# Two graph-attention layers: layer 1's probabilities turned by DMA blocks and VectorE instead of TensorE

## The chip, the cores and the metric

The kernel runs on one core of a Trainium2 chip, in one launch. The time is the device time of that core in microseconds (us), the median of several executions. One further execution was taken by the hardware profiler; its page and trace are what this text reads. Engines are named as in the profile: PE is TensorE, DVE is VectorE, ACT is ScalarE, POOL is GpSimd, and SP is the engine that issues DMAs.

## The reference, cut to what matters

The input is 128 graphs of 64 nodes with 768 features, and a 0/1 adjacency per graph. Layer 0 is a 12-head graph attention with a gate; the change doesn't touch it. Layer 1 is a 6-head self-attention, masked by the adjacency, with head size 128:

```python
def _L1_gnn_ref(seq_inputs, Wq, bq, Wk, bk, Wv, bv, Wf, bf, graph_mask):
    q = _heads(seq_inputs @ Wq + bq)
    k = _heads(seq_inputs @ Wk + bk)
    v = _heads(seq_inputs @ Wv + bv)
    scores = jnp.einsum('bhqd,bhkd->bhqk', q, k) / np.sqrt(HEAD_SIZE)
    bias = jnp.where(graph_mask, 0.0, NEG)[:, None]
    probs = jax.nn.softmax(scores + bias, axis=-1)
    ctx = jnp.einsum('bhqk,bhkd->bhqd', probs, v)
    ctx = ctx.transpose(0, 2, 1, 3).reshape(...)
    return ctx @ Wf + bf
...
x = _layernorm(x + _L1_gnn_ref(x, ..., adj), axis=-1)
```

Everything is float32. The softmax comes out with the query node on the partitions. For the contexts TensorE sums over the key node, so the probabilities are needed with the key node on the partitions: they must be transposed, 64 by 64 for each graph and head.

## The kernel before, in words

**Tiles.** A tile is two graphs, 128 rows. There are 64 tiles, 32 pairs of tiles, and in layer 1 16 groups of two pairs (four tiles). Within a group, q (0 or 1) is the pair and i (0 or 1) the tile of the pair. Layer 0 (`phase_a`) runs first and leaves in DRAM, for each tile, its output `x1_d`, the same transposed (`xT_d`), and layer 1's values `v_d`. Then `phase_b` does layer 1.

**Dense products.** The four large products use a bilinear algorithm with 15 half-size products: `STEPS` lists 15 steps, each with two float32 products of 128 by 128 by 256, which the profile shows as four MATMULs of line 428. A `Stream` object holds one such pass. In each step VectorE (line 1205 for q and k, 1222 for the last product) or ScalarE (line 1200) adds the partial sum from PSUM to its outputs. PSUM has four buffers for this (`psX`) and four more for everything else in the layer (`psb`).

**Order of the work.** There is no planner at run time. `phase_b` puts closures into a dictionary under a step number, `run` calls them in that order, and each engine's instruction queue, and SP's queue of DMAs, is filled in just this order. An instruction waits on semaphores for its inputs and buffers; what stands behind it on the same engine waits with it. Step numbers are therefore positions in the queues, not times, and an engine that has little to do runs ahead.

**One window.** Group g starts at step o = 90 g. In 90 steps the queue holds 15 steps of q for even heads, 15 of k for even heads, 15 of q and 15 of k for odd heads (steps o to o+59, `start_qk`), and the output product of the group before (steps o+60 to o+89, `start_f`, 15 for each pair). After step o+62 stand the scores (line 1244), read out by VectorE with the mask added (line 1253). The softmax of group g runs in the window of group g+1: with o' = o + 90, it starts at step `sm` = o' + 5. For tile (q, i) the start is t = sm + 3 i + 8 q, and then

- t: row maximum (line 1265), t+1: subtraction (1284), both on VectorE
- t+3: exponential on ScalarE (1287), t+6: row sum on VectorE (1291)
- t+7: reciprocal on VectorE (1295) and scaling on GpSimd (`sm_scale`, line 1296), in place
- t+4: the four DMAs that load this tile's values from `v_d` (`load_v`, line 1159), into one of three places of `xb`, taken in turn, so that the fourth tile's load waits for the contexts of the first pair
- t+10: `probs`: three TensorE transposes of 128 by 128 into PSUM (line 1302) and a ScalarE copy to SBUF, into `pt` (line 1308)
- t+12, for i = 1: `contexts` of the pair: 192 small matmuls (line 1326), then four VectorE reads that add the bias of v (line 1340).

From the contexts GpSimd forms the eleven sums that the output product needs (`pair_sum`, line 1190), from step sm + 18 for the first pair. The last group has no following window; it uses its own schedule, with the exponential per head on ScalarE.

**Tiles' places.** q and k of a group are held in two tiles each (`start_qk`, name with `bufs=2`), one for even and one for odd heads; the scores read them at step o+62. The next group's k for odd heads is written from step o'+45 on.

**DMAs.** All of layer 1's DMAs stand in SP's queue. SP issues them one after the other; if one must wait, SP waits. Stores of the finished x (line 1356) wait for ScalarE's normalization; loads of x (1166), of the transposed input (485) and of the adjacency (1144) stand there too.

Of the kernel before, what the change touches and what calls it, by code (L numbers as in the profile page):

```python
# [10 lines left out]
F32 = mybir.dt.float32  # L11
U8 = mybir.dt.uint8
AF = mybir.ActivationFunctionType
ALU = mybir.AluOpType
AX = mybir.AxisListType

P = 128
# [204 lines left out]
def kernel(  # L222
# [31 lines left out]
    nc = tc.nc  # L254
# [869 lines left out]
    def phase_b(ctx, wq, wk, early_sums):  # L1124
# [11 lines left out]
        DUP = {0: 0, 2: 1, 4: 2, 5: 3}  # L1136
        bv_v = bv_c.rearrange("p (j h) -> p j h", h=2)
        st = [dict() for _ in range(NG)]

        def load_adj(g):  # L1140
            d = st[g]
# [51 lines left out]

        def start_qk(d, name, w, bias, j):

            o = k1.tile([P, 6, 2, P], F32, name=name, bufs=2)

            def first(b, positive, ps):
                hd = 2 * (b % 3) + j
                nc.scalar.activation(  # L1200
                    o[:, b], ps, AF.Identity, bias=bias[:, hd : hd + 1], scale=1.0 if positive else -1.0
                )

            def add(b, positive, ps):
                nc.vector.tensor_tensor(o[:, b], o[:, b], ps, ALU.add if positive else ALU.subtract)  # L1205

            d[name] = Stream(
                lambda r, slot, c: w[:, slot, c, j * P : (j + 1) * P],
                lambda r, slot, c: (
                    dup[:, DUP[r]] if d is st[0] and r in DUP else group_part(d, r)  # L1210
                )[:, :, c, :],
                [P, 2, P],
                first,
                add,
            )
            d[name + "T", j] = o
# [33 lines left out]
        def scores_read(d, nb):  # L1250
            for q in range(2):
                for i in range(2):
                    nc.vector.scalar_tensor_tensor(
                        d["s"][q][:, i, 2 * nb : 2 * nb + 2, :], d["pc", nb][:, q, i],
                        1.0 / math.sqrt(DH),
                        d["fill"][:, q, i, None, :].to_broadcast([P, 2, S]),
                        op0=ALU.mult, op1=ALU.add,
                    )
# [34 lines left out]
        def sm_scale(d, q, i):  # L1293
            s, rs = sm_part(d, q, i), small.tile([P, HEADS], F32, name="rs1")
            nc.vector.reciprocal(rs, d["sm", q, i])
            nc.gpsimd.tensor_tensor(s, s, rs[:, :, None].to_broadcast([P, HEADS, S]), ALU.mult)

        def probs(d, q, i):

            ps = psb.tile([P, CH, P], F32, name="pb")  # L1300
            for j in range(CH):
                nc.tensor.transpose(  # L1302
                    ps[:, j, :],
                    d["s"][q][:, i, 2 * j : 2 * j + 2, :].rearrange("p h m -> p (h m)"),
                    ident,
                )
            d["pt", i] = spare[i].rearrange("p (c n) -> p c n", n=P)
            nc.scalar.copy(d["pt", i], ps)

        def contexts(d, q):  # L1310
            pcs = [context(d, q, i) for i in range(2)]
# [100 lines left out]
        for g in range(NG):  # L1412
            d, o = st[g], N * g
            d["S"] = {} if g else early_sums
            last = g == NG - 1
            if g:
                at(o - 29 if g > 1 else 14, lambda g=g: load_T4(g))
                at(o - 35, lambda g=g: load_adj(g))
            at(o + 26, lambda d=d: fill(d))
            ready = {}  # L1420
            for k in sorted(range(len(SUMS)), key=need) if g == 0 else range(len(SUMS)):

                if g == 0:

                    if k > 3:
                        at(max(int(need(k)) - 5, 0), lambda d=d, k=k: sum_of_group(d, k, nc.vector))
                    continue
                if g == 1:

                    t = max([R * 3 + SUM_STEPS[k] + 2] + [ready[r] for r in SUMS[k][:2] if r in ready])  # L1430
                    ready[6 + k] = t
                else:
                    t = o - 24 + 2 * k
                at(t, lambda d=d, k=k: sum_of_group(d, k, nc.gpsimd))
            if g == 0:
                for r, n in DUP.items():
                    nc.scalar.copy(dup[:, n], group_part(d, r))
            for j in range(2):
                for n, (name, w, bias) in enumerate((("q", wq, bq_c), ("k", wk, bk_c))):
                    b0 = o + (2 * j + n) * R  # L1440
                    at_first(b0, lambda d=d, a=(name, w, bias, j): start_qk(d, *a))
                    for i in range(R):
                        at_first(b0 + i, lambda d=d, name=name, i=i: d[name].step(i))
            b0 = o + 4 * R + 2
            at(b0, lambda d=d: scores(d))
            for nb in range(3):
                at(b0 + 1 + (1 if last else 2) * nb, lambda d=d, nb=nb: scores_read(d, nb))

            sm = o + 4 * R + 6 if last else o + N + 5
            for q in range(2):  # L1450
                f = o + ((6 if last else 10) + q) * R
                for i in range(2):

                    t = sm + 4 * i + 13 * q if last else sm + 3 * i + 8 * q
                    at(t + (2 if last else 4), lambda g=g, q=q, i=i: load_v(g, q, i))
                    if last:
                        at(t, lambda d=d, q=q, i=i: sm_top(d, q, i, True))
                        at(t + 2, lambda d=d, q=q, i=i: sm_top_exp(d, q, i))
                        at(t + 5, lambda d=d, q=q, i=i: sm_scale_act(d, q, i))
                        at(t + 8, lambda d=d, q=q, i=i: probs(d, q, i))  # L1460
                        if i:
                            at(t + 11, lambda d=d, q=q: contexts(d, q))
                        continue
                    at(t, lambda d=d, q=q, i=i: sm_top(d, q, i))
                    at(t + 1, lambda d=d, q=q, i=i: sm_sub(d, q, i))
                    at(t + 3, lambda d=d, q=q, i=i: sm_exp(d, q, i))
                    at(t + 6, lambda d=d, q=q, i=i: sm_total(d, q, i))
                    at(t + 7, lambda d=d, q=q, i=i: sm_scale(d, q, i))
                    at(t + 10, lambda d=d, q=q, i=i: probs(d, q, i))
                    if i:  # L1470
                        at(t + 12, lambda d=d, q=q: contexts(d, q))

                pr = sm + (6 + 13 * q if last else 8 + 8 * q)
                ready = {}
                for k in range(len(SUMS)):
                    if q == 0:
                        t = pr + 10 + (k if last else 2 * k)
                    else:

                        t = max(  # L1480
                            [f - R + SUM_STEPS[k] + 1, pr + 10]
                            + [ready[r] for r in SUMS[k][:2] if r in ready]
                        )
                        ready[6 + k] = t
                    at(t, lambda d=d, q=q, k=k: pair_sum(d, q, k))
                at(f - (3 if last else 12), lambda g=g, q=q: load_x(g, q))
                at(f - (1 if last else 8), lambda d=d, q=q: add_bf(d, q))
                at_first(f, lambda d=d, q=q: start_f(d, q))
                for i in range(R):
                    at_first(f + i, lambda d=d, q=q, i=i: d["F", q].step(i))  # L1490
                if last and q:
                    for b in range(6):
                        t = f + max(i for i in range(R) if STEPS[i][5][b])
                        at(t, lambda d=d, b=b: end_stats(d, b))

                    at(f + R - 2, lambda d=d: end_top(d, 1))
                    at(f + R - 1, lambda d=d: end_top(d, 0))
                    at(f + R - 1, lambda g=g, d=d: end_norm(g, d, 1))
                    at(f + R - 1, lambda g=g, d=d: end_norm(g, d, 0))
                    continue  # L1500
                for i in range(2):
                    t = f + R + 1 + 2 * i
                    at(t, lambda d=d, q=q, i=i: norm1(d, q, i))
                    at(t + 1, lambda d=d, q=q, i=i: norm2(d, q, i))

                    at(t + 4 + 2 * i, lambda d=d, q=q, i=i: norm3(d, q, i))
                    at(t + 6 + 2 * i, lambda g=g, d=d, q=q, i=i: store(g, d, q, i))
            if g == 0:
                at(16, lambda: load_adj(0))
                bf_bc = rows(k1, bf, "bf_bc")  # L1510
# [40 lines left out]
```

## Time and profile before

| what | value |
|---|---|
| median of 3 executions | 2821.89 us (2819.24 to 2822.54) |
| profiled execution, its own time | 2821.93 us |
| span of the profiled execution | 2820.1 us, mean granted clock of TensorE 0.995 |
| busy share: PE, DVE, ACT, POOL | 98%, 68%, 41%, 53% |
| layer 1, one window: length, PE busy | 85.73 us, all of it |
| line 1302, transposes of layer 1 | 192 instructions, 273 ns each |
| line 1308, copies from PSUM | 64 instructions, 478 ns each |
| line 1296, scaling on GpSimd | 60 instructions, 828 ns each |

The span runs from the first to the last instruction; the execution's own time is 1.8 us longer, and stands within 0.1 us of the median. A matmul's duration in the profile overlaps that of the next one, so what an instruction costs TensorE is read from the distance between starts. The DMA records give for each DMA the start and length of its issue on SP, the start of each packet, and the moments at which its parts completed.

### The profile page before, as it was taken

To read this page: it belongs to the slowest core of one execution; us is meant where nothing else is said; L and a number is where in the kernel's file an instruction comes from. 1 tells how busy PE (TensorE), PEld (TensorE's weight loads), DVE (VectorE), ACT (ScalarE), POOL (GpSimd) and SP (SyncE) were. 2 spreads that over 40 slices of the span, in tenths; PEclk is the share of its full clock that TensorE was granted. 3 is DMA by queue.
4 is the path that set the end of the run, shared out by engine and by line. 5 is a ranking of instruction groups with operands and counts; after the bars stand their busy time and mean duration, and the time that the engine had idled before them with its cause. 6 is when DMAs were issued, how large, how long until landed. Compare 5 with 4: busy or idle time off the path is not lost.

```text
span 2820.1 us, 50020 instructions
## 1 busy us (share of the span) xinstructions
PE 2775.9 (98%) x17544; PEld 1958.7 (69%) x17544; DVE 1905.0 (68%) x4026; ACT 1163.1 (41%) x3685; POOL 1495.9 (53%) x1791
## 2 busy tenths in 40 slices
PE   8899999999999999999799999999999999999998
PEld 7445545555555555555578888888888888888887
DVE  4888888888888888888754555555555555555556
ACT  4466565665666665665622221122221222211223
POOL 1656556555555565565455645445645445554455
PEclk9999999999999999999899999999999999999999
DMA  5454454454454454444631221221221222211222
GB/s 147 126 151 136 136 152 130 133 154 131 133 157 134 133 150 132 140 150 132 174 130 35 91 81 65 70 91 58 91 73 63 80 65 84 91 68 58 91 85 74
DMA packets 358682, 308.36 MB, mean 109 GB/s; under 512 B 226592, under 2 KB 304160, under 8 KB 358432
## 3 DMA queue, kind: packets, MB, share of 16 engines
q1 hardware_dynamic: 358144, 304.77, 35.2%
q8 instruction: 140, 2.29, 0.3%
q14 instruction: 110, 0.90, 0.1%
q10 hardware_dynamic: 288, 0.39, 0.0%
HBM read 191.41 MB, written 101.06 MB: 104 GB/s over the span
## 4 chain that ended last, share of the span: by engine, by line
PE 93%; DVE 3%; DMA 1%; POOL 1%; ACT 1%; SPq 0%; issue 0%; POOLq 0%; DVEq 0%; ACTq 0%
PE X L428 70%; PE X L373 15%; PE pa L901 2%; PE pb L1326 2%; PE pb L1244 2%; PE pa L883 1%; PE pb L1302 1%; PE X L715 1%; PE X L700 1%; POOL Sc L1190 0%; DMA w<-in_L_gnn_Wv_dram 0%; DVE s L853 0%; ACT s L862 0%; DMA hb_bc<-in_L_gnn_H_b_dram 0%; DVE T L634 0%
## 5 line engine op out<-in xcount | busy, mean ns | idle before, releaser
L428 PE MATMUL X<-S,w 128*128 128x256 f32 x2752 | 636.5, 380 | 0.0
L428 PE MATMUL X<-w,S 128*128 128x512 f32 (+1 forms) x1364 | 598.9, 584 | 10.7 <-POOL S L668 7.5
L428 PEld LDWEIGHTS X<-S,w 128*128 128x128 f32 x2752 | 519.1, 190 | 68.5
L428 PEld LDWEIGHTS X<-w,S 128*128 128x128 f32 x1364 | 254.9, 191 | 289.8 <-issue 241.0
L1222 DVE TENSOR_TENSOR xs<-xs,X 128x256 f32<-128x256 f32 x512 | 209.6, 418 | 175.1 <-PE X L428 166.9
L872 POOL TENSOR_TENSOR s<-s,rs 128x384 f32<-128x384 f32 x128 | 106.9, 836 | 372.1 <-DVE rs L870 355.9
L428 PE MATMUL X<-w,Sc 128*128 128x256 f32 x1280 | 294.4, 381 | 0.1
L1205 DVE TENSOR_TENSOR k<-k,X 128x256 f32<-128x256 f32 x320 | 132.6, 417 | 232.4 <-PE X L428 160.6
L373 PE MATMUL X<-w,S 128*128 128x384 f32 x768 | 270.9, 490 | 1.5 <-POOL S L456 1.4
L428 PEld LDWEIGHTS X<-w,Sc 128*128 128x128 f32 x1280 | 241.5, 190 | 34.1 <-DVE xs L1222 0.9
L1205 DVE TENSOR_TENSOR q<-q,X 128x256 f32<-128x256 f32 x320 | 132.9, 419 | 195.0 <-PE X L428 155.0
L428 PE MATMUL X<-xb,w 128*128 128x256 f32 x1024 | 258.6, 383 | 0.8 <-ACT q L1200 0.8
L862 ACT ACTIVATE s<-s,nmx 128x64 f32<-128x64 f32 x768 | 254.8, 335 | 6.8 <-DVE nmx L857 6.8
L516 ACT ACTIVATE xs<-xs,shift,rstd 128x768 f32<-128x768 f32 x62 | 63.5, 1025 | 435.8 <-POOL shift L512 416.0
L428 PE MATMUL X<-w,T 128*128 128x512 f32 (+1 forms) x496 | 223.9, 583 | 5.7 <-DVE xb L757 3.4
L1200 ACT ACTIVATE k<-X,bk_c 128x256 f32<-128x256 f32 x192 | 90.9, 473 | 316.4 <-PE X L428 316.4
L846 ACT ACTIVATE s<-s,src 128x64 f32<-128x64 f32 x768 | 196.6, 338 | 37.6 <-DMA s<-dst_d 34.2
L428 PEld LDWEIGHTS X<-xb,w 128*128 128x128 f32 x1024 | 192.2, 190 | 28.4 <-ACT q L1200 1.2
L757 DVE TENSOR_TENSOR hgp<-hgp,X 128x512 f32<-128x512 f32 (+1 forms) x235 | 150.6, 651 | 80.8 <-PE X L428 67.2
L1200 ACT ACTIVATE q<-X,bq_c 128x256 f32<-128x256 f32 x192 | 90.8, 473 | 276.7 <-PE X L428 276.7
L373 PEld LDWEIGHTS X<-w,S 128*128 128x128 f32 x768 | 141.1, 190 | 90.1 <-POOL S L456 1.6
L1190 POOL TENSOR_TENSOR w<-cT 128x256 f32<-128x256 f32 x32 | 23.3, 727 | 334.2 <-PE X L428 332.9
(143 smaller groups left out, 4893.1 us busy)
## 6 DMA issues: line engine op xcount, KB each, us to landing
xb<-in_x_dram SPq DMA_DIRECT2D x64, 384.0 KB
s<-dst_d SPq DMA_DIRECT2D x128, 192.0 KB
x_d<-xb SPq DMA_DIRECT2D x64, 384.0 KB
xT_d<-T SPq DMA_DIRECT2D x64, 384.0 KB
v_d<-v SPq DMA_DIRECT2D x128, 192.0 KB
xb<-xT_d SPq DMA_DIRECT2D x32, 768.0 KB
xb<-v_d SPq DMA_DIRECT2D x256, 96.0 KB
xs<-x_d SPq DMA_DIRECT2D x64, 384.0 KB
```

The costliest lines, as they stand in the source:

```text
L373: nc.tensor.matmul(o, self.lhsT(i, c), rhs, start=first and c == 0, stop=last and c == CH - 1, skip_group_check=True,)
L428: nc.tensor.matmul(ps, self.lhsT(r, slot, c), self.rhs(r, slot, c), start=start and c == 0, stop=stop and c == 1, skip_group_check=True,)
L516: nc.scalar.activation(r, r, AF.Identity, bias=shift, scale=rstd)
L757: nc.vector.tensor_tensor(o, o, view(ps), ALU.add if positive else ALU.subtract)
L846: nc.scalar.activation(self.s[:, a], self.s[:, a], AF.Prelu, bias=self.src[:, a : a + 1], alpha=LEAKY_ALPHA,)
L862: nc.scalar.activation(self.s[:, a], self.s[:, a], AF.Exp, bias=self.nmx[:, a : a + 1], accum_out=self.sm[:, a : a + 1],)
L872: nc.gpsimd.tensor_tensor(t, t, rs[:, :, None].to_broadcast([P, A // 2, S]), ALU.mult)
L901: nc.tensor.matmul(self.pos[h2][own, j, :], self.pt[rws, j, own], rhs, start=True, stop=True,)
L1200: nc.scalar.activation(o[:, b], ps, AF.Identity, bias=bias[:, hd : hd + 1], scale=1.0 if positive else -1.0)
L1205: nc.vector.tensor_tensor(o[:, b], o[:, b], ps, ALU.add if positive else ALU.subtract)
L1222: nc.vector.tensor_tensor(o, o, ps, ALU.add if positive else ALU.subtract)
L1244: nc.tensor.matmul(pc[own, q, i, j, :], qT[:, b, q, own], kT[:, b, q, own], start=True, stop=True,)
```

## The change: what it does

The transposition is taken apart into two moves. A 64-by-64 transposition is four 32-by-32 blocks, each transposed in itself, with the two off-diagonal blocks changing places. VectorE transposes 32-by-32 blocks inside a group of 32 partitions (`nc.vector.transpose`); bringing blocks to other partitions is left to DMA, by way of a DRAM tile.

For the groups 0 to 14 (the last one keeps the old way):

- `scores_read` writes the heads in another order (slot h*3 + j instead of 2j + h), so that the blocks of one half are contiguous.
- `sm_scale` writes its product to a new place, `turned`, with the two halves of the key nodes outermost.
- `probs` is replaced by `probs_out` at t+10: one DMA of 192 KB from `turned` to the DRAM tile `p_d`, in 512 runs of 384 bytes, and four DMAs of 48 KB back into `blocked`, each to 32 partitions in 128 runs of 384 bytes; and by `probs_turn` at t+20: one VectorE transposition of 128 by 384 from `blocked` into `pt`. The three TensorE transposes and the ScalarE copy are gone.
- `contexts` moves from t+12 to t+22. With t now sm + 3 i + 11 q, the first pair's contexts move from o'+20 to o'+30, the second's from o'+28 to o'+41. The pair sums move with them.
- `load_v` no longer follows t: the first three tiles are loaded at sm, sm+1 and sm+2, the fourth at sm+26.
- `turned` and `blocked`, two of each, lie in the tile that holds k for odd heads (`late`), which is free from step o+62 until the next group's k for odd heads is written.

```diff
+        late = k1.tile([P, 6, 2, P], F32, name="k1")
+        parts = late.rearrange("p b q n -> p (b q n)").rearrange("p (t f) -> p t f", t=4)
+        turned = [parts[:, i].rearrange("p (b h m) -> p b h m", b=2, m=32) for i in range(2)]
+        p_d = [spill.tile([4, P, CH * 32], F32, name=f"p_d{i}") for i in range(2)]
+        blocked = [parts[:, 2 + i].rearrange("p (g j m) -> p g j m", g=4, m=32) for i in range(2)]
...
-            o = k1.tile([P, 6, 2, P], F32, name=name, bufs=2)
+            o = late if (name, j) == ("k", 1) else k1.tile([P, 6, 2, P], F32, name=name + str(j))
...
         def scores_read(d, nb):
             for q in range(2):
                 for i in range(2):
+                    own = d["s"][q][:, i]
                     nc.vector.scalar_tensor_tensor(
-                        d["s"][q][:, i, 2 * nb : 2 * nb + 2, :], d["pc", nb][:, q, i],
+                        own[:, 2 * nb : 2 * nb + 2, :] if d is st[-1]
+                        else own.rearrange("p (h j) m -> p h j m", h=2)[:, :, nb],
+                        d["pc", nb][:, q, i],
...
         def sm_scale(d, q, i):
             s, rs = sm_part(d, q, i), small.tile([P, HEADS], F32, name="rs1")
             nc.vector.reciprocal(rs, d["sm", q, i])
-            nc.gpsimd.tensor_tensor(s, s, rs[:, :, None].to_broadcast([P, HEADS, S]), ALU.mult)
+            d["sn", i] = turned[i]
+            nc.gpsimd.tensor_tensor(
+                turned[i].rearrange("p b h m -> p h b m"),
+                s.rearrange("p h (b m) -> p h b m", b=2),
+                rs[:, :, None, None].to_broadcast([P, HEADS, 2, 32]),
+                ALU.mult,
+            )
...
+        def probs_out(d, q, i):
+
+            nc.sync.dma_start(
+                p_d[i].rearrange("q p x -> p q x"),
+                d["sn", i].rearrange("p b (h j) m -> p (b h) (j m)", h=2),
+            )
+            for h in range(2):
+                for b in range(2):
+                    o = 32 * (2 * h + b)
+                    nc.sync.dma_start(
+                        blocked[i][o : o + 32].rearrange("p g j m -> p g (j m)"),
+                        p_d[i][2 * b + h].rearrange("(g n) x -> n g x", g=4),
+                    )
+
+        def probs_turn(d, i):
+            d["pt", i] = spare[i].rearrange("p (c n) -> p c n", n=P)
+            nc.vector.transpose(
+                d["pt", i].rearrange("p c (g n) -> p c g n", g=4),
+                blocked[i].rearrange("p g j m -> p j g m"),
+            )
...
-                    t = sm + 4 * i + 13 * q if last else sm + 3 * i + 8 * q
-                    at(t + (2 if last else 4), lambda g=g, q=q, i=i: load_v(g, q, i))
+                    t = sm + 4 * i + 13 * q if last else sm + 3 * i + 11 * q
+                    at(t + 2 if last else sm + (2 * q + i if 2 * q + i < 3 else 26), lambda g=g, q=q, i=i: load_v(g, q, i))
...
-                    at(t + 10, lambda d=d, q=q, i=i: probs(d, q, i))
+                    at(t + 10, lambda d=d, q=q, i=i: probs_out(d, q, i))
+                    at(t + 20, lambda d=d, i=i: probs_turn(d, i))
                     if i:
-                        at(t + 12, lambda d=d, q=q: contexts(d, q))
-
-                pr = sm + (6 + 13 * q if last else 8 + 8 * q)
+                        at(t + 22, lambda d=d, q=q: contexts(d, q))
+
+                pr = sm + (6 + 13 * q if last else 18 + 11 * q)
```

## The prediction

> **What bounds the kernel now.** First the page: TensorE is busy for 98% of the span and carries 93% of the chain that ended last.
>
> ```profile
> span 2820.1 us, 50020 instructions
> PE 2775.9 (98%) x17544; PEld 1958.7 (69%) x17544; DVE 1905.0 (68%) x4026; ACT 1163.1 (41%) x3685; POOL 1495.9 (53%) x1791
> ```
>
> A mean over both layers says little, so next a table of stretches of layer 1 (length, busy time by engine, clock, DMA share, GB/s), and the chain, from which I take the scores of two successive groups.
>
> ```profile
> 1772.00:1858.00 86.00, 86.00 (x693) 75.46 (x687) 46.82 (x126) 18.64 (x36) 43.34 (x53) 1.00 0.22 75
> ...
> 2154.95 2.95 PE pb L1244 x96
> ...
> 2240.68 2.95 PE pb L1244 x96
> ```
>
> In layer 1 PE never idles, and a window is 2240.68 - 2154.95 = 85.73 us. So PE time removed there is gained in full, if nothing makes PE wait. The timeline of PE shows what a `probs` costs it:
>
> ```profile
> 2108.47 1.03 PE L428 MATMUL X<-S,w 128*128 128x256 f32 x4
> 2109.33 0.49 PE L1302 MATMUL pb<-ident,s 128*128 128x128 f32 x3
> 2109.66 1.03 PE L428 MATMUL X<-S,w 128*128 128x256 f32 x4
> ...
> 2114.40 1.65 PE L1326 MATMUL pb<-w,xb 64*64 64x64 f32 x96
> 2115.99 1.13 PE L428 MATMUL X<-xb,w 128*128 128x256 f32 x4
> ```
>
> Start to start, three transposes cost 2109.66 - 2109.33 = 0.33 us, though listed at 0.273 us each. The contexts cost 1.68 us with the gap before them. A step is 0.868 us (37.32 us for 172 MATMULs in the chain). Check: 90 x 0.868 + 2.95 + 2 x 1.68 + 4 x 0.33 = 85.75 us.
>
> Then SP and GpSimd, in the timelines of DMA issues and of POOL:
>
> ```profile
> 2102.47 2.48 SPq L1159 DMA_DIRECT2D xb<-v_d  x4
> 2105.05 0.54 SPq L1356 DMA_DIRECT2D out_dram<-xs  x1
> ...
> 2108.04 0.83 POOL L1296 TENSOR_TENSOR s<-s,rs 128x384 f32<-128x384 f32 x1 [5.19 <-DVE rs L1295]
> ```
>
> Four small loads keep SP busy for 2.48 us: issue is a price of its own. And layer 0 has the new VectorE operation, at 0.684 us:
>
> ```profile
> L634 DVE STREAM_TRANSPOSE T<-xp x248: 649/684/774, 26.3 to 1403.4; 128x384 f32<-128x384 f32 x124
> ```
>
> **What the Trainium skill says.** "VectorE: DVE Perf Modes", The three transpose paths: VectorE transposes within 32-by-32 blocks only, hence the DMAs. "DMA: Bandwidth & Descriptors", Two DMAs through the same engine are not ordered: a DMA reading what another wrote must be issued after the first one's completion. The trace agrees: at 1367.13 us the `dst_d` read-back in layer 0 is issued 0.05 us after the write's last completion record. Same page, Anatomy of one DMA (told there for GpSimd's path): about 2.0 us are fixed, mostly completion, and waits are done on the issuing sequencer. The trace has 1.88 us (median) from issue to last completion for the 192 KB store of v. "Runtime: NRT & Kernel Launch", Instruction fetch mechanics: instructions come in 16 KiB blocks, mostly hidden. Not quite here: the records have 67 packets of 16384 bytes between 1600 and 2700 us, about 1.0 us each, and nearly every DMA issue that takes over 0.9 us, after the first 10 us of the span, lies on one.
>
> **Removed.** 15 groups x 4 tiles x 0.33 = 19.8 us of PE. Also 60 ScalarE copies, 60 x 0.478 = 28.7 us, on an engine busy 18.6 of 86 us: nothing.
>
> **Added off PE.** VectorE gets 4 x 0.684 = 2.7 us a window, on 47 of 86 busy. The work itself is covered; its waiting may not be. Scores and scaling keep their counts and sizes; GpSimd's scattered output I take at 0.83 us, at most 1.0 (from line 1190, 0.73 for 256 elements, scaled gives 1.1).
>
> **The chain through SP.** I count u from the window's step 0, 2108.47 - 15 x 0.868 = 2095.45. GpSimd ends the first scaling at 2108.87, u = 13.4. SP's earlier items (two value loads ahead of time, a store at 6.6, a third load, a store until about 10.1) are through. Now each tile needs one DMA out, a wait, and four in, and SP can do nothing else meanwhile, since the ins stand behind the wait and the next tile's out behind them.
>
> - Out: 512 runs of 384 bytes. No such DMA is in the trace. Those with several runs per partition issue in 0.60 us and start packets after 1.3 (plain stores 0.34 and 0.83). 384 runs of 256 bytes land 2.43 us after issue when quiet (tenth percentile, line 832); 128 runs more, at 16 engines and some 30 ns, add 0.24: 2.7 us. Ends: 2.35 (256 runs, quiet), 3.4 (line 832's busy median; the same DMA page's Specifications say that under 512 bytes a read-modify-write is done, of which the 128-byte stores show nothing).
> - In: four issues, 2.53 us by line 1159; the last starts 1.9 us after the first and lands 2.2 later.
> - Waits: 0.07.
>
> A tile thus takes P = 2.7 + 0.07 + 2.53 = 5.3 us of SP. Outs start at u = 13.5, 18.8, 24.1, 29.4 (the second pair's scalings, now about 23.0 and 25.2, are earlier), and SP reaches the fourth value load at 34.7.
>
> **When it is needed.** Step s ends at 0.868(s+1), plus 1.68 after the first contexts.
>
> - Second tile: landed 18.8 + 2.77 + 1.9 + 2.2 = 25.7. VectorE reaches its transposition (step 28) about 0.7 after the step, at 25.9; done 26.6. The contexts (step 30) start at 26.9. In time by 0.3.
> - Fourth tile: landed 36.3; VectorE at 36.4 + 0.7 = 37.1. In time.
> - Fourth value load: its last DMA starts 34.7 + 1.9 = 36.6, lands 2.45 later (quiet 2.35, median 2.59): 39.05. The second contexts start at 38.1, and their second half, which needs it, at 38.1 + 0.33 + 0.68 = 39.1. In time by nothing.
> - Instruction fetches: one per 16.4 us, so 1.55 in these 25.5 us; I estimate 0.7 of them to strike and each to delay by 0.6: 0.65 us.
>
> So the value load comes at 39.7 on average, 0.6 us late; averaging only the positive part over a spread of 0.8 us, w = 0.7 us of PE waiting per window. Sum: 2821.9 - 19.8 + 15 x 0.7 = 2812.6, say 2812.5 us. Each 0.1 us on P moves w by 0.4, the time by 6 us.
>
> **Moved, and why at nothing.** The pair sums start after the contexts' reads, at 28.6 + 2 = 30.6; eleven of 0.73 end at 39, and are needed at step 60, u = 55.5. The loads of x stand behind the fourth value load, issue after 37.3, land about 5 later; with two additions of 1.8 us that is 46 at most, against 55. Were that cover gone, each us would be a us of PE. The next k for odd heads enters `late` at step 45, u = 43.3, after the last transposition at 37.8; 5.5 us of cover. The `blocked` tiles are rewritten by ins at 26.8 and 32.2, after the transpositions at 23 and 26.6. Behind VectorE's waiting transposition stand the evictions of the next steps; an accumulator returns after three steps, so a wait of a us there is absorbed, two are not.
>
> **Rivals.**
>
> 1. *Hidden altogether.* If the out lands in 2.35 us, P is 4.95, and the value load comes at 37.7 before fetches. For it: SP-only waits and a quiet DMA system (DMA share 0.22). Against: 512 runs. It gives 2802.
> 2. *Slower.* The round trip is longer, and the value load behind four of them makes PE wait more than it saved. For: short runs to DRAM, no instance in the trace, four in series on one queue. Against: DMAs are light. w passes 1.32 (break-even) at P near 5.5; at 5.75, w is about 2.4: 2821.9 - 19.8 + 36 = 2838. At the upper end, 3.4 us out (P = 6.0), the loss is about 30.
> 3. *Break-even*, P between 5.4 and 5.57: 2816 to 2827.
>
> The change not taking effect is no case: line 1302 keeps 12 of its 192.
>
> **How the numbers follow.** About 0.2% (5.6 us) is what a measurement of this kernel can tell from no change. Chances: partly late 0.42 (2808 to 2816); hidden 0.20 (2800 to 2808); break-even 0.13; slower 0.25 (2827.5 to 2853). Faster is 0.62, same 0.13, slower 0.25. The range, 2801 to 2838, leaves out some 0.05 below and 0.12 above.
>
> **What would show it.** Windows of about 85.1 us (84.4 if hidden, over 85.7 if slower); PE idle just before line 1326, released by DMA; SP busy without a break from u = 13.5 to 37, five DMAs every 5.3 us. Wrong, if the out's landing is far from 2.7 us, if idle stands before line 428 instead, or if VectorE waits for its transposition by over a us.

## The result, and the profile after

The changed kernel takes 2801.18 us (median of 6, 2796.68 to 2803.29) against 2820.15 us (median of 6, 2816.38 to 2822.54) for the kernel before, measured beside it. The ratio is 0.9934, with a 95% interval of 0.9924 to 0.9944: 19.0 us faster. The forecast was 2812.5 us, in a range of 2801 to 2838: it had the sign right, half of the gain, and the wrong case as the likeliest. What came is its first rival, the trip hidden altogether (2802 us). The median lies 0.2 us inside the range, less than its executions scatter.

The page of the kernel after, its span and busy time by engine:

```profile
span 2794.9 us, 50230 instructions
PE 2754.2 (99%) x17364; PEld 1940.4 (69%) x17364; DVE 1924.3 (69%) x4086; ACT 1140.0 (41%) x3625; POOL 1500.9 (54%) x1791
```

PE has 180 instructions fewer, DVE 60 more and ACT 60 fewer, as the change says. The same view as before of one stretch of layer 1 (start and end; length; busy time of PE, PE's weight loads, DVE, ACT and POOL; granted clock; DMA share; GB/s), and the scores of three groups from the chain:

```profile
1753.80:1838.20 84.40, 84.40 (x650) 74.06 (x649) 48.37 (x130) 17.10 (x33) 43.05 (x53) 1.00 0.29 93
...
2054.09 2.95 PE pb L1249 x96
...
2138.51 2.95 PE pb L1249 x96
...
2222.91 2.95 PE pb L1249 x96
```

A window is now 2222.91 - 2138.51 = 84.40 us instead of 85.73, and PE still never idles in it. The difference, 1.33 us, is the four times 0.33 us of the transposes. From the first scores to the last, the profiled execution went from 1262.7 to 1242.9 us, 19.8 us less. The two spans differ by 25.2 us; 5.8 us of that lie before the first scores, nearly all of it in layer 0, which the change doesn't touch and where executions scatter: the profiled executions of all the runs here begin their first scores between 1486.4 and 1492.2 us.

Now the part that the forecast turned on. The timeline of DMA issues in one window (start, length, line, destination from source, how many; `k<-p_d` and `p_d<-k` name the tile in which `turned` and `blocked` lie):

```profile
2087.34 2.48 SPq L1164 DMA_DIRECT2D xb<-v_d  x4
2089.92 0.54 SPq L1391 DMA_DIRECT2D out_dram<-xs  x1
2093.75 0.38 SPq L1326 DMA_DIRECT2D p_d<-k  x1
2095.97 1.75 SPq L1333 DMA_DIRECT2D k<-p_d  x4
2097.82 0.38 SPq L1326 DMA_DIRECT2D p_d<-k  x1
2100.05 1.73 SPq L1333 DMA_DIRECT2D k<-p_d  x4
2102.89 0.38 SPq L1326 DMA_DIRECT2D p_d<-k  x1
2105.26 1.74 SPq L1333 DMA_DIRECT2D k<-p_d  x4
2107.16 0.38 SPq L1326 DMA_DIRECT2D p_d<-k  x1
2109.45 1.73 SPq L1333 DMA_DIRECT2D k<-p_d  x4
2111.28 3.08 SPq L1164 DMA_DIRECT2D xb<-v_d  x4
```

With the window's step 0 at 2080.4, the first out starts at u = 13.35 (13.5 in the forecast). Two outs follow each other by 2097.82 - 2093.75 = 4.07 us, not 5.3. The third waits for GpSimd, not for SP: its scaling ends at 2102.86, 0.03 us before it. The fourth value load starts at 31, not 34.7. And what needs these, in the timelines of PE (96 matmuls for the contexts of a pair, not the 192 named further up) and of DVE in the same window:

```profile
2107.24 1.65 PE L1361 MATMUL pb<-w,xb 64*64 64x64 f32 x96
...
2118.51 1.67 PE L1361 MATMUL pb<-w,xb 64*64 64x64 f32 x96
```

```profile
2105.96 0.57 DVE L1340 STREAM_TRANSPOSE w<-k 128x384 f32<-128x384 f32 x1
...
2117.23 0.57 DVE L1340 STREAM_TRANSPOSE w<-k 128x384 f32<-128x384 f32 x1
```

The contexts start at u = 26.86 and 38.13 (26.9 and 38.1 forecast) and wait for nothing. Over the 15 windows, the second tile's blocks have landed 1.4 to 2.8 us before VectorE takes them, the fourth value load 1.9 to 3.4 us before its matmuls start (median 35.9 against 38.9).

### The profile page after: what moved, and what is told of

It reads as the page before. It is cut to its first block, busy times and chain, and to the rows that moved or that the text cites. A ratio compares the mean times of both kernels' runs of the same rounds, so it can differ in the third digit from the quotient of the medians.

```text
span 2794.9 us, 50230 instructions
## 1 busy us (share of the span) xinstructions
PE 2754.2 (99%) x17364; PEld 1940.4 (69%) x17364; DVE 1924.3 (69%) x4086; ACT 1140.0 (41%) x3625; POOL 1500.9 (54%) x1791
## 4 chain that ended last, share of the span: by engine, by line
PE 94%; DVE 2%; POOL 1%; DMA 1%; ACT 1%; issue 1%; SPq 0%; POOLq 0%; DVEq 0%; ACTq 0%
PE X L428 71%; PE X L373 14%; PE pa L901 2%; PE pb L1361 2%; PE pb L1249 2%; PE pa L883 1%; PE X L715 1%; PE X L700 1%; PE X L686 0%; DMA w<-in_L_gnn_Wv_dram 0%; DMA xb<-xT_d 0%; DMA hgp<-in_L_gnn_W_dram 0%; POOL Sc L1195 0%; ACT s L862 0%; DVE w L331 0%
## 5 line engine op out<-in xcount | busy, mean ns | idle before, releaser
L373 PE MATMUL X<-w,T 128*128 128x384 f32 x576 | 198.5, 490 | 0.6 <-DVE T L634 0.3
```

Of the source, the lines that this page charges most:

```text
L373: nc.tensor.matmul(o, self.lhsT(i, c), rhs, start=first and c == 0, stop=last and c == CH - 1, skip_group_check=True,)
```

## The experiments

The theory (A, in the expectations): the gain is the TensorE time of the transposes alone, and the trip is hidden as long as SP's turn per tile leaves the value load and the blocks in time. Rivals: the later placement brings the gain (B), the trip costs something even so (C), SP's turn doesn't decide (D). Windows below are means over fourteen windows of the profiled execution, from the second scores to the last; the kernel before has 85.73 us, the one after 84.41. In the edits, which are against the changed kernel, `...` stands for code left out. Waits inside the contexts are listed some 0.2 us shorter than the time they cost: a small matmul is listed with 0.22 us, but undisturbed the next one starts 0.02 us after it.

**The new schedule with the old transposes.**

```diff
...
-                turned[i].rearrange("p b h m -> p h b m"),
...
+            nc.gpsimd.tensor_tensor(s, s, rs[:, :, None].to_broadcast([P, HEADS, S]), ALU.mult)
...
-                    at(t + 10, lambda d=d, q=q, i=i: probs_out(d, q, i))
-                    at(t + 20, lambda d=d, i=i: probs_turn(d, i))
+                    at(t + 20, lambda d=d, q=q, i=i: probs(d, q, i))
```

> The changed kernel's schedule (contexts at o'+30 and o'+41, value loads at sm, sm+1, sm+2 and sm+26), but the probabilities transposed on TensorE as before. Theory A, the gain is the 0.33 us of TensorE per tile that the transposes cost, and the rest is hidden: 2820 us (2817 to 2823), windows of 85.72 us. Theory B, the gain or a part of it comes from placing the contexts later and loading the values earlier: 2801 to 2812 us.

Measured 2818.08 us, ratio to before 0.9996 (0.9988 to 1.0005), windows of 85.72 us. Its chain shows the distance between scores:

```profile
2063.93 2.95 PE pb L1249 x96
...
2149.66 2.95 PE pb L1249 x96
```

85.73 us, as before. Theory B has fallen: placing the contexts later brings nothing by itself.

**The trip left out.**

```diff
-            nc.sync.dma_start(p_d[i]..., d["sn", i]...)
-            for h in range(2): for b in range(2): nc.sync.dma_start(blocked[i]..., p_d[i]...)
...
-                blocked[i].rearrange("p g j m -> p j g m"),
+                d["sn", i].rearrange("p b (h j) m -> p j (b h) m", h=2),
```

> The changed kernel without the trip through DRAM: the five DMAs per tile are left out, and VectorE's block transposition reads GpSimd's output directly, so that no block changes partitions and the output differs. Theory A, the trip is hidden whole: 2801 us (2798 to 2804), windows of 84.40 us as with the trip. Theory C, the trip still costs something in the changed kernel, by SP, by the DMA engines or by VectorE's order: under 2798 us.

Measured 2800.83 us (2798.21 to 2801.70), windows of 84.40 us: the same as with the trip. Its 300 DMAs cost the changed kernel nothing that can be measured; C has fallen.

**Eight DMAs back instead of four.**

```diff
-                    nc.sync.dma_start(blocked[i][o : o + 32]..., p_d[i][2 * b + h]...)
+                    for k in range(2):
+                        g2 = slice(2 * k, 2 * k + 2)
+                        nc.sync.dma_start(blocked[i][o : o + 32, g2]..., p_d[i][2 * b + h]...[:, g2])
```

> The changed kernel with each of the four DMAs back cut in two: the same bytes, eight issues per tile. Theory A with the sum of the prediction: SP's turn per tile grows from 4.1 to 2.2 + 0.05 + 8 x 0.44 = 5.75 us, the fourth value load lands at u = 24.9 + 11.5 + 4.4 = 40.8 and is needed at 38.9, so TensorE waits some 1.9 us per window: windows near 86.3 us, 2829 us (2820 to 2838). Theory D, SP's turn is not what decides and there is room beyond it: 2801 us.

Measured 2897.85 us, ratio 1.0271 (1.0256 to 1.0287), windows of 90.6 us. That is slower, where D said no change; but theory A had it at 28 us more than the changed kernel, and it is 97. The place was right: the timeline of PE shows it waiting inside the second pair's contexts for the value load.

```profile
2166.54 0.93 PE L1363 MATMUL pb<-w,xb 64*64 64x64 f32 x48
2169.19 0.29 PE L1363 MATMUL pb<-w,xb 64*64 64x64 f32 x2 [1.72 <-DMA xb<-v_d]
2170.50 1.98 PE L1363 MATMUL pb<-w,xb 64*64 64x64 f32 x46 [1.02 <-DMA xb<-v_d]
2172.41 2.07 PE L428 MATMUL X<-S,w 128*128 128x256 f32 x4
2174.28 3.17 PE L428 MATMUL X<-xb,w 128*128 128x256 f32 x8
```

The last two lines show a second loss: four MATMULs of a step take 1.87 us from start to start there, instead of 0.86. The table of stretches has the reason in its clock column (after the five engines' busy times):

```profile
2160.00:2168.00 8.00, 7.46 (x79) 6.27 (x77) 2.24 (x5) 1.63 (x4) 4.40 (x7) 1.00 0.25 60
2168.00:2176.00 8.00, 5.65 (x57) 4.54 (x58) 3.59 (x8) 0.00 (x0) 3.52 (x3) 0.63 0.50 154
```

After the waits PE is granted half its clock. Between 1560 and 2760 us this happens eleven times, for 3.41 or 6.83 us each, 54.6 us in all, which costs up to half of that. The kernels before and after have none there. The Trainium skill, "TensorE: Matmul & The Clock Gate", Part 1, states the halving after an idle window of about 3.4 us; here two or three waits that came to 1.8 to 3.1 us within such a stretch were enough (the last section has the count).

The waits are the larger loss all the same. From the first scores to the last this execution takes 93.6 us more than the changed kernel. The clock is halved there for 64.9 us, up to 32 us of loss; the rest, some 61 us or 4.1 a window, is waiting, against the 1.9 expected: the value load lands at a median of u = 43.5, not 40.8.

**Transposition and contexts six steps earlier.**

```diff
-                    at(t + 20, lambda d=d, i=i: probs_turn(d, i))
+                    at(t + 14, lambda d=d, i=i: probs_turn(d, i))
-                        at(t + 22, lambda d=d, q=q: contexts(d, q))
+                        at(t + 16, lambda d=d, q=q: contexts(d, q))
```

> The changed kernel with VectorE's transposition at t+14 and the contexts at t+16, six steps (5.2 us) earlier each; the DMAs stay where they are. Theory A: the second tile's blocks land at u = 23.2 as before, the contexts would start at 21.7 and start at 24.0, so 2.3 us of waiting; the second pair's chain moves with it, and its value load comes 1.9 us late: 4.2 us per window at most, windows of 86.7 to 88.6 us, 2835 to 2864 us. Theory D, the later placement isn't needed: 2801 us.

Measured 2908.53 us, ratio 1.0313 (1.0298 to 1.0328), windows of 92.2 us: beyond the expected upper end, with the clock halved for 71.7 us between 1560 and 2760 us, up to 36 us of loss. The later placement brings nothing alone, but with six steps of it gone the trip isn't hidden.

**Seven DMAs back: the turn that the forecast took as likeliest.** As with eight, but one of the four stays whole:

```diff
+                    n = 4 if (h, b) == (1, 1) else 2
+                    for k in range(0, 4, n):
+                        g2 = slice(k, k + n)
```

> The changed kernel with three of the four DMAs back cut in two: seven issues per tile, SP's turn 2.2 + 0.05 + 7 x 0.44 = 5.3 us, which is the turn that the prediction took as the likeliest. Theory A, the prediction's sum was right and only the turn was mis-sized: the value load lands at u = 39.2 and is needed at 38.9, a wait of 0.3 us, with fetches about 0.7 us: windows of 84.7 to 85.2 us, 2806 to 2813 us. Theory F, a wait of TensorE costs more than itself, since its clock drops to half for some 3.4 or 6.8 us after waits of 1 to 3 us (as in the runs with eight DMAs and with contexts six steps earlier), and small waits are enough for it: windows of 86.4 us or more, 2830 us or more.

Measured 2856.66 us, ratio 1.0130 (1.0115 to 1.0145), windows of 88.5 us. SP's turn is 5.40 us for the first tile (median of the windows). The value load lands at a median of u = 41.6, not 39.2. The timeline of DMA issues, here from a window's second tile on, shows trips growing on the way:

```profile
2125.04 0.43 SPq L1326 DMA_DIRECT2D p_d<-k  x1
2127.31 4.12 SPq L1336 DMA_DIRECT2D k<-p_d  x7
2131.47 0.43 SPq L1326 DMA_DIRECT2D p_d<-k  x1
2134.10 4.09 SPq L1336 DMA_DIRECT2D k<-p_d  x7
2138.23 0.43 SPq L1326 DMA_DIRECT2D p_d<-k  x1
2140.53 3.12 SPq L1336 DMA_DIRECT2D k<-p_d  x7
```

Seven issues take 3.12 us where nothing disturbs, and 4.1 twice: in each of the two, one issue of 1.37 and 1.39 us coincides with a packet of 16384 bytes of the instruction queue (starting at 2127.78 and 2135.45). From the first scores to the last this execution takes 59.9 us more than the changed kernel; the clock was halved ten times, 41 us in all, which is up to 20 us of it; the rest, some 39 us or 2.6 us a window, is waiting. Theory F had the time right, but the halved clock that it named is only a third of the loss; theory A's sum had the waiting too small and the clock not at all.

**Six DMAs back.** Two of the four stay whole (`n = 4 if h else 2`).

> The changed kernel with two of the four DMAs back cut in two: six issues per tile, SP's turn 4.9 us, the value load at u = 37.5 against 38.9. Both theories A and F: still hidden, windows of 84.4 us, 2801 us (2798 to 2804). A time over 2806 us would say that the room is smaller than the trace of the changed kernel shows.

Measured 2812.58 us, ratio 0.9974 (0.9968 to 0.9981), windows of 85.1 us. The expectation missed: the value load lands at a median of 39.6, 0.1 to 1.95 us after its matmuls could start (the last of its four DMAs, which the first matmuls don't need), where the sum without disturbances gives 37.5. The profiled execution is the fastest of the twenty (2807.67 us); from the first scores to the last it takes 10.3 us more than the changed kernel, and from start to start all of it is lost inside the contexts. Its waits of PE between 1600 and 2700 us, where no halving occurs (what waited, for what; us in total, times, longest):

```profile
PE pb L1364 <- DMA xb<-v_d: 4.4, 11, 0.8
```

**Two, and four, steps earlier.** As with six steps, with t+18 and t+20, and with t+16 and t+18.

> The changed kernel with VectorE's transposition and the contexts two steps (1.74 us) earlier. Theory A: the second tile's blocks (u = 23.2) against VectorE at 23.8, the value load (35.9) against 37.1: still hidden but for single windows, 84.4 to 84.6 us, 2801 to 2804 us. Theory F: the same, but a single window that waits may cost several us: up to 2810 us.

> The changed kernel with VectorE's transposition and the contexts four steps (3.47 us) earlier. Theory A: the first contexts could start at u = 23.4, their probabilities are there at 23.95; 0.6 us of waiting, and about 0.45 us for the value load: 1.0 us per window, 85.4 us, 2816 us. Theory F: the clock drops in most windows, 1.7 to 3.4 us more each: 87 to 89 us, 2840 to 2867 us.

Two steps: 2804.27 us, ratio 0.9945 (0.9931 to 0.9960), windows of 84.40 us but for a few up to 85.6: at the upper end of theory A, and no halving. Four steps: 2827.59 us, ratio 1.0034 (1.0024 to 1.0045), windows of 86.2 us. Here theory F was wrong on the clock: in the profiled execution it doesn't drop between 1560 and 2760 us, though PE waits in every window. From the first scores to the last it takes 26 us more than the changed kernel. Theory A was right on the kind, low on the size (1.0 us per window, 1.8 measured).

**Seven DMAs back, without the fourth value load.**

```diff
+            if g < NG - 1 and 2 * q + i == 3:
+                st[g]["v", q, i] = st[g]["v", q, 0]
+                return
```

> The kernel with seven DMAs back per tile, but without the fourth tile's value load in the groups 0 to 14: the fourth tile's contexts read the third tile's values, so the output differs. Theory G, what TensorE waits for first is the value load that stands behind the four trips in SP's queue, not the probabilities: with it gone, only the second and fourth tile's blocks can be late, by some 0.2 to 0.5 us: windows of 84.5 to 85.2 us without a drop of the clock, 2803 to 2813 us. Theory H, the probabilities themselves are late and the load is late only with them: 2840 us or more, as with the load (2856.7).

Measured 2808.07 us, ratio 0.9950 (0.9934 to 0.9967), windows of 85.1 us, no drop of the clock. With the load it is 2856.66. The waits of PE between 1600 and 2700 us, with the load and then without it:

```profile
PE pb L1364 <- DMA xb<-v_d: 21.1, 25, 2.1
PE pb L1364 <- DVE w L1343: 3.2, 3, 1.6
PE pb L1364 <- DVE q L1210: 1.6, 2, 1.0
PE pb L1364 <- PE pb L1364: 0.3, 1, 0.3
```

```profile
PE pb L1367 <- DVE w L1346: 5.0, 7, 1.5
PE pb L1367 <- PE pb L1367: 1.0, 2, 0.6
```

Theory G holds: it is the value load, standing last in SP's queue, that makes TensorE wait first; the probabilities (`w` from VectorE) come second, with single waits up to 1.5 us, longer than the 0.2 to 0.5 us expected.

**Issues of three runs and of one.** In the first tile of each pair the DMAs back are cut into `slice(0, 3)` and `slice(3, 4)`.

> The changed kernel, with each DMA back of the first tile of a pair cut into one of three runs and one of one run per partition; the second tile's stay at four runs. A measurement of the issue alone. Theory I, three runs are what makes an issue long (0.60 us for the value loads with three runs of 64 partitions, 0.42 us for the DMAs back with four of 32): issues of 0.55 us or more for three runs, 0.42 for four. Theory J, the runs don't matter: all near 0.42 us, and the value loads' 0.60 us has another cause. In both the time stays below 2815 us: the first tiles' turn grows to 5.6 to 5.9 us, the second's stays 4.1, and the value load comes at 38.6 to 39.2.

Issues took 0.42 us for three runs, 0.43 for one, 0.42 for four (medians), while the value loads stayed at 0.60: theory J. Between one and four runs on 32 partitions the number makes no difference, so that their three runs alone don't make the value loads' issue long. This kernel took 2816.45 us in one execution, a little over the bound expected; PE waited 6.9 us for the value load, and the clock dropped twice.

## Why the prediction was right and wrong

- **Removed, 19.8 us: right.** 1262.7 - 1242.9 = 19.8 us, and with the old transposes in the new schedule nothing is gained.
- **When it is needed: right.** The contexts' starts came within 0.05 us of the forecast, the second half of the second contexts at 38.9 (39.1). The first out came at 13.35 (13.5).
- **VectorE, GpSimd and the moved work at nothing: right.** The transposition takes 0.57 us (0.684 assumed), the scaling 0.83. The waits the change could bring show no cost.
- **SP's turn, P = 5.3 us: this term failed.** It was made of 2.7 us for the out, 0.07 and 2.53 for four issues. Measured: 2.18 us from the out's issue to its last completion (median; issue 0.38), and 1.75 us for four issues of 0.42. So P is 4.07. The out had been built up from DMAs with an issue of 0.60 and a late first packet, and the ins were priced by the value loads; neither row was of the same shape. The DMAs back also land 1.87 us after their issue, not 2.2. Even the lower end of the out in the forecast (2.35) was too slow. Whether the read-modify-write that the forecast named is part of the 2.18 us, these durations can't tell: the store of v, with runs of 1536 bytes and a quarter as many, takes 1.96 (median of all 128; the forecast had 1.88).
- **w = 0.7 us: fell with it.** With P = 4.07 the value load is in time by 1.9 us or more in all windows, and w is 0.
- **Instruction fetches, 0.65 us: too small.** With six DMAs back, undisturbed issues give 13.4 + 4 x 5.0 + 4.4 = 37.8 for the value load, and 39.6 is measured: 1.8 us. Most of that goes with the fetches: from each first out to the last value load, over 15 windows, 25 of the distances from issue to issue are more than 0.4 us longer than the shortest in the same place, and 24 of these 25 overlap a packet of 16384 bytes, while only 38 of all the 465 distances do. Those 38 hold 24.0 of the 28.3 us by which all together exceed the shortest, 1.6 us a window. No run took the fetches away, so this is a coincidence in time, not an experiment. The room in the changed kernel covers it.
- **The price of being late, "each 0.1 us on P moves w by 0.4, the time by 6 us": too mild.** At the turn that the forecast had assumed (5.4 us measured), the kernel isn't at 2812.5 but at 2856.66 us, and from six to seven DMAs back each 0.1 us on P costs some 11 us. Of what it loses against the changed kernel, waiting is two thirds and the halved clock up to one third; layer 1 of the kernel before, where PE never waits, couldn't show the clock, but the seam between the layers could have: there PE waits, and the clock granted from 1300 to 1450 us is 0.93. The break-even in P was put near 5.5; it lies between 5.0 (six DMAs, 2812.58) and 5.4 (seven). The second rival's mechanism, the value load behind four trips, was thus real, and nearer and steeper than stated.

So the forecast's direction came out of a sum whose errors pointed apart: a turn too long on one side, fetches and a price of lateness too low on the other. In part that was luck, and so are the 0.2 us by which the median lies inside the range.

## What to carry to other kernels

Where TensorE is the bound, as here, moving its transposes to DMA and VectorE gained just their start-to-start time, because every later step had a place late enough; the schedule is what makes the round trip free, though it gains nothing alone. Count the whole queue: the transfer that comes last may be one that has nothing to do with the change and only stands behind it. And price a DMA by a row of its own shape, or keep both ends open, because near the edge 1.3 us more of SP's turn per tile (4.07 against 5.40) lie between 19 us gained and 37 us lost.

## What the runs showed of the hardware that was not expected

- A short wait of TensorE can cost more than itself, and where it falls decides. In each trace here all changes of the clock after the first 100 us lie on one grid of 3.4133 us, to within 0.005 us. In layer 1, over all the traces up to the last scores, the clock was halved 39 times, each time at the end of a step of this grid in which PE had idled for 1.32 to 3.12 us, mostly in two or three waits. Of the steps at full clock with 1.3 to 1.85 us of idling, 15 were followed by half the clock and 15 were not; the 24 with more all were. With four steps earlier, no step idles for more than 1.61 us, and the clock never dropped.
- The same is seen between the layers: a single wait of 2.66 us in the kernel before (from 1339.24 us) lies within one step of the grid, and the clock is halved for 3.41 us after it; in the kernel after, the same wait (from 1334.89 us) is cut by the end of a step, and no halving follows. What decides between 1.3 and 1.85 us stays open.
- A store of 192 KB to DRAM in 512 runs of 384 bytes lands in 2.18 us, only 0.2 us later than the 192 KB store of v in 128 runs (1.96 us, median).
- The issue of a DMA on SP takes 0.42 us for 32 partitions with one to four runs of 384 bytes, 0.60 for 64 partitions with three of 512. But layer 0's loads of eight such runs to 32 partitions take 0.61, so the number of runs isn't excluded beyond four; whether the partitions, the run length, the total or the source's pattern make the difference is open.
